# Work behind a unit's sums gets a smaller key in a list scheduler (four-layer graph network, one core)

## The chip, the cores and the metric

The kernel runs on one core of one Trainium2 chip. Five engines work from instruction queues of their own: TensorE (PE in the profile, with PEld for its weight loads), VectorE (DVE), ScalarE (ACT), GpSimd (POOL) and SyncE (SP), which here only issues DMAs. The metric is the device time of one launch, in microseconds (us). Six runs of the kernel before gave a median of 3188.3 us (3178.14 to 3199.47).

## The reference, cut to what matters

A batch of 8 graphs shares one adjacency matrix of 2048 nodes: random, symmetric, with every node its own neighbour, about 17 neighbours a node. Each node has 128 features in float32. Four layers follow each other: attention, graph, attention, graph.

```python
# layers 0 and 2 (8 heads of 16)
Q, K, V = h @ Wq, h @ Wk, h @ Wv
attn = softmax(where(adj == 0, -inf, Q K^T / sqrt(16)))
x = layer_norm(h + (attn V) @ Wo + bo, ln1_g, ln1_b)
x = layer_norm(x + relu(x @ W1 + b1) @ W2 + b2, ln2_g, ln2_b)   # 128 -> 256 -> 128
# layers 1 and 3
h = x @ W
e = leaky_relu((h @ a_src)[i] + (h @ a_dst)[j], 0.2)
y = softmax(where(adj == 0, -inf, e)) @ h + x
x = ln_gamma * (y - mean(y)) * rsqrt(var(y) + 1e-5) + ln_beta
```

## The kernel before, in words

**Tiling.** The 2048 nodes are cut into 32 units of 64 nodes. A unit's neighbours are never multiplied as a full matrix: their rows are fetched from a table in DRAM, five steps `t` a unit (TG = 5; four steps of two tiles of 128 neighbour rows, one step of a single tile). A row of the table holds what a neighbour gives in the next layer for all eight batches (K and V in attention; h and its score in a graph layer). The eight batches lie in two halves of four, on the upper and lower rows or side by side.

**An attention unit** (`attention`, L1693). For each of its five steps: POOL issues the gather of the neighbour rows into a `kv` buffer (L1671, six buffers); PE spreads the queries to the neighbour rows with a 0/1 matrix `hot` (L1734, into `qe`); DVE multiplies them with K (L1746) and reduces by head (L1753); ACT takes the exponential (L1763); the V rows are weighed with it, on POOL or for some steps on DVE (L1773, "weighing"); PE adds the weighed rows and the weights up by node, again with `hot` (L1805, into `acc` and `sums`). This add is the last reader of the `kv` buffer.

**Behind a unit's sums** (`after_attention`, L1855). DVE inverts the sums (L1863, L1864) and divides (L1870). Then: four transposes on PE (`ps_t`, L1482), a copy on ACT (L1471), the product with Wo (`ps_o`, L1505), the residual add on DVE (L1882), centring on PE (`ps_c`, L1495), squares on ACT (L1607), the root (L1617, L1618), the normalised rows (L1640), transposes and scale (`x1`, L1650), the product with W1 in two parts (`ps_f`, ReLU at L1902), the product with W2 (`ps_y`, L1912), the second residual add and a second norm, and the layer's result `xnew`. `keep` stores it to DRAM (SP, L1359). `project` multiplies it with the next layer's weights (`ps_p`, L1533 and L1535), copies the rows out (L1471), adds a small score strip on DVE (L1573) and stores the rows to the next layer's table (SP, L1593).

**A graph unit** (`graph`, L1932) gathers in the same way, scores on DVE (L1971, L1978), exponential on ACT (L1983), builds weights on DVE (L1993) and adds up on PE (L2009). Behind its sums (`after_graph`, L2068) come the inverse, a scale, the centred residual (L2099), one norm, and either store and projection for the next layer or, in the last layer, the store of the output (L2120).

**Before a unit** `fetch` (L1366) loads x (L1371) and, in an attention layer, the compressed `hot` rows (L1386) through SP; ACT unpacks them (L1393).

**What sets the order.** No order is written out by hand. Every piece of work is an `op` with its cost per engine, a key, and the buffers that it reads and writes. `Plan.order` (L670) simulates the engines: whenever one is free in that simulation, it takes the ready op with the smallest key, if a buffer is free for it. Buffers of the tags `kv`, `hot`, `x`, `q_sb` and `acc` go out strictly by key. Ops are issued in the order found, so every engine and every DMA queue has one fixed program order on the chip. All products but the sums and the spreads share two PSUM buffers (tag `m`). POOL's and DVE's weighings can't both be planned with the shared port.

**The keys.** A unit's base is 1000 x layer + 5 x unit. In an attention unit, step t has key = base + t: gather and spread at key - 6, exponential at key - 4, multiply, reduce and add at key, weighing at key + 1.5. The fetch is at base - 12, the unpacking at base - 8, the queries at base - 4. In a graph unit the gather is at key - 12, the score at key - 1, the exponential at key - 4. Inverse and division are at base. Everything behind them is at `key` as set by the line that the change touches, the two residual adds and the roots at `key - 2`.

**The seams between layers.** A gather of layer n + 1 needs the stored table rows of layer n. In a graph layer the first four units do the steps of paired tiles first; these gathers read only rows of units 0 to 29, the others wait for units 30 and 31 too. Unit 31 does the work behind its sums in two halves of two batches.

**Layer 0** also builds the lists of neighbours from the adjacency matrix, until about unit 20, beside its attention.

Of the kernel before, what the change touches and what calls it, by code (L numbers as in the profile page):

```python
# [34 lines left out]
TG = 5  # L35
# [564 lines left out]
class Plan:  # L600
# [36 lines left out]
    def op(self, costs, fn, key, reads=(), writes=(), joins=(), holds=(), shares=(), port=False, dma=0):  # L637


        o = Op({e: us * self.share for e, us in costs.items()}, fn, key, port, dma)  # L640
        shares = [*shares, *(c.whole for c in (*reads, *writes, *joins, *holds) if c.whole)]
        before = set()
        for c in reads:
            before.update(c.writers)
        for c in writes:
            before.update(c.writers)
            before.update(c.readers)
        for c in joins:
            before.update(c.readers)
        for c in reads:  # L650
            c.readers.append(o)
        for c in writes:
            c.writers, c.readers = [o], []
        for c in joins:
            c.writers.append(o)
        before.update(w for c in holds for w in [c.owner, *c.writers] if w)
        for c in dict.fromkeys([*writes, *joins, *reads, *holds, *shares]):
            if c.tag:
                if not c.owner:
                    c.owner = o  # L660
                    o.allocs.append(c)
                c.left += 1
                o.cells.append(c)
        for b in before:
            b.next.append(o)
        o.waits = len(before)
        o.behind = [c.owner for c in (*shares, *joins) if c.tag and c.owner is not o]
        self.ops.append(o)
# [96 lines left out]
def flat(ap):  # L765
    return ap if len(ap.shape) == 2 else ap.rearrange("p b d -> p (b d)")


class Sparse:
# [1085 lines left out]
    def after_attention(self, n, u, acc, sums, x, base):  # L1855
        L, hb = self.layers[n], self.HB
        op, count, cols = self.op, len(self.blocks), self.columns
        key = base + TG
        heads = slice(self.blocks.start * H, self.blocks.stop * H)
        rc = self.rows("rc", [P, hb * H], 1, H)  # L1860

        def inverse(e):
            e.tensor_scalar(rc.tile, sums.tile[:, heads], 1e-30, None, ALU.max)  # L1863
            e.reciprocal(rc.tile, rc.tile)  # L1864

        op({"DVE": 0.5}, inverse, base, reads=[sums], writes=[rc])
        a = self.rows("rows", [P, hb, P], 1, 1, name="a")

        def divide(e):
            e.tensor_tensor(  # L1870
                a.tile.rearrange("p b (h d) -> p (b h) d", d=HD),
                acc.tile[:, cols].rearrange("p (c d) -> p c d", d=HD),
                rc.tile.unsqueeze(2).to_broadcast([P, count * H, HD]),
                ALU.mult,
            )

        op({"DVE": 0.65}, divide, base, reads=[acc, rc], writes=[a])

        def add_to(r, ps, bias, other, key, of=lambda t: t):
            op(  # L1880
                {"DVE": 0.72},
                lambda e: e.scalar_tensor_tensor(r.tile, ps.tile, bias, of(other.tile), ALU.add, ALU.add),  # L1882
                key,
                reads=[ps, other],
                writes=[r],
            )

        at = self.rows("at", [P, CH], 1, P)
        ps = self.transposed(a, key, at)
        op(self.either(0.6, 0.68), lambda e, ps=ps: self.copy(e, at.tile, ps.tile), key, reads=[ps], writes=[at])  # L1890
        r = self.rows("r", [P, CH], 1, P, name="r1")
        ps = self.product(L["Wo"], at, key, "ps_o", r)
        add_to(r, ps, L["bo"], x, key - 2, lambda t: t[:, cols])
        normed = self.norm(self.centred(r, key), key)
        x1 = self.scaled(normed, L["ln1_g"], L["ln1_b"], "x1", key)
        hidden = self.rows("hidden", [P, FFN // P, CH], 2, P)
        for f in range(FFN // P):
            ps = self.product(L["W1"][:, f * P : (f + 1) * P], x1, key, "ps_f", hidden)

            def relu(e, f=f, ps=ps):  # L1900
                if e is self.nc.scalar:
                    e.activation(hidden.tile[:, f, :], ps.tile, AF.Relu, bias=L["b1"][:, f : f + 1])  # L1902
                else:
                    e.tensor_scalar(hidden.tile[:, f, :], ps.tile, L["b1"][:, f : f + 1], 0.0, ALU.add, ALU.max)

            op(self.either(0.7, 0.68), relu, key, reads=[ps], joins=[hidden])
        r = self.rows("r", [P, CH], 1, P, name="r2")
        ps = self.bank("ps_y")
        for f in range(FFN // P):
            op(  # L1910
                {"PE": 1.0},
                lambda e, f=f, ps=ps: e.matmul(  # L1912
                    ps.tile,
                    lhsT=L["W2"][:, f, :],
                    rhs=hidden.tile[:, f, :],
                    start=(f == 0),
                    stop=(f == FFN // P - 1),
                ),
                key,
                reads=[hidden],  # L1920
                writes=[ps],
                holds=[r],
            )
        add_to(r, ps, L["b2"], x1, key - 2)
        normed = self.norm(self.centred(r, key), key)
        x = self.scaled(normed, L["ln2_g"], L["ln2_b"], "xnew", key)
        self.keep(u, x, key)
        self.project(n + 1, u, x, key)
# [139 lines left out]
    def after_graph(self, n, u, outs, banks, acc, x, base):  # L2068
        L, hb = self.layers[n], self.HB
        op, cols, blocks = self.op, self.columns, self.blocks  # L2070
        key = base + TG

        rc = self.rows("rc", [P, hb], 1, 1, name="rcg")
        used = banks[blocks.start // 2 : blocks.stop // 2]
        outs = outs[blocks.start // 2 : blocks.stop // 2] if len(outs) > 1 else outs

        def inverse(e):
            for k, bank in enumerate(used):
                sums = bank()[:, 0 : 2 * (P + 1)].rearrange("p (b d) -> p b d", b=2)[:, :, P]
                e.tensor_scalar(rc.tile[:, 2 * k : 2 * k + 2], sums, 1e-30, None, ALU.max)  # L2080
            e.reciprocal(rc.tile, rc.tile)

        op({"DVE": 0.5}, inverse, base, reads=outs, writes=[rc])
        a = self.rows("rows", [P, hb, P], 1, 1, name="a")
        for k, b in enumerate(blocks):
            op(
                self.either(0.37, 0.28),
                lambda e, b=b, k=k: self.scale(e, a.tile[:, k, :], acc(b)[:, 0:P], rc.tile[:, k : k + 1]),
                base,
                reads=[*outs, rc],  # L2090
                joins=[a],
            )
        r = self.rows("r", [P, CH], 1, P)
        mine = x if self.made is None else Part(x, lambda t: t[:, cols])
        mine.writers = x.writers
        ps = self.centred(mine, key, r, a)
        op(
            {"DVE": 0.65},
            lambda e: e.tensor_tensor(r.tile, ps.tile, flat(a.tile), ALU.add),  # L2099
            key - 2,  # L2100
            reads=[ps, a],
            writes=[r],
        )
        normed = self.norm(r, key)
        if n < len(LAYERS) - 1:
            x = self.scaled(normed, L["ln_gamma"], L["ln_beta"], "xnew", key)
            self.keep(u, x, key)
            self.project(n + 1, u, x, key)
        else:

            def last(e):
                shape = [P, len(blocks), P]
                e.tensor_tensor(normed.tile, normed.tile, L["ln_gamma"].unsqueeze(1).to_broadcast(shape), ALU.mult)
                e.tensor_tensor(normed.tile, normed.tile, L["ln_beta"].unsqueeze(1).to_broadcast(shape), ALU.add)

            op({"POOL": 2.4, "DVE": 1.2}, last, key, writes=[normed], port=True)

            op(
                {"SP": 0.45},
                lambda e: e.dma_start(out=self.out[u][:, cols], in_=flat(normed.tile)),  # L2120
                key,
                reads=[normed],
                dma=P * P * 4 * len(blocks),
            )
# [105 lines left out]
```

## Time and profile before

| what | value |
| --- | --- |
| median of six runs | 3188.3 us (3178.14 to 3199.47) |
| the profiled execution: its time, its span | 3180.48 us, 3178.5 us |
| busy share of the span: PE, PEld, DVE, ACT, POOL | 76%, 44%, 72%, 45%, 67% |
| mean granted TensorE clock | 0.879 |
| moved by DMA | 1022.52 MB, mean 322 GB/s |
| gathers (POOL's queue), share of the 16 DMA engines | 72.8% |
| SP's queue, the same | 13.3% |

The times by stage follow from the traces of the gathers: layer 0 from 0 to about 1100 us, layer 1 to about 1655, layer 2 to about 2605, layer 3 to the end.

```profile
span 3178.5 us, 59465 instructions
...
DVE  7799889998889834444446888888988984555555
...
DMA  8788888999999769999987898999989967998994
...
L1671 POOL DMA_INDIRECT kv<-table,idx x1152 | 1196.6, 1039 | 826.2 <-issue 348.8
L1773 POOL TENSOR_TENSOR kv<-kv 128x2048 f32<-128x2048 f32 x260 | 921.1, 3555 | 63.9 <-ACT kv L1763 59.5
L1746 DVE TENSOR_TENSOR kv<-qe,kv 128x2048 f32<-128x2048 f32 (+1 forms) x320 | 662.0, 2069 | 114.4 <-DMA kv<-table,idx 60.8
L1753 DVE TENSOR_REDUCE s<-kv 128x128 f32<-128x2048 f32 (+1 forms) x320 | 659.6, 2061 | 9.0 <-DVE kv L1746 0.5
```

How to read it: the two rows of digits cut the span into 40 slices of 79.5 us; a digit is the busy share of the slice in tenths. DVE's row shows the four layers: 8 and 9 in the two attention layers, 4 and 5 in the two graph layers, where DMA's row has mostly 9. The last four lines are groups of instructions: line, engine, operation, what it writes and reads, count; then busy time, mean of one in ns; then the time its engine stood still just before them, and what ended most of it. DVE spends 1321.6 us of its 2302.6 us in the multiplies and reduces of the attention layers.

### The profile page before, as it was taken

The numbers are of one execution on the slowest core, as the hardware profiler recorded it, in microseconds if no ns is written. First come the engines' busy times: TensorE is split into PE (matmuls) and PEld (weight loads), VectorE is DVE, ScalarE is ACT, GpSimd is POOL, SyncE is SP. The second block draws the span as 40 slices with busy tenths as digits, with TensorE's granted clock in tenths as the row PEclk, the third lists the DMA queues.
The fourth block names the chain that finished last, engine by engine and source line by source line (L and its number), as shares of the span: only waits on it lengthen the run. The fifth ranks groups of instructions, "written<-read, shape, count | busy, mean of one in ns | idle before, by whom it ended". The sixth has DMA issues, their size and how long they took to land.

```text
span 3178.5 us, 59465 instructions
## 1 busy us (share of the span) xinstructions
PE 2419.4 (76%) x21668; PEld 1391.8 (44%) x21668; DVE 2302.6 (72%) x3783; ACT 1416.2 (45%) x4899; POOL 2130.9 (67%) x1456
## 2 busy tenths in 40 slices
PE   6667777777888758888885788788888786767774
PEld 4323333333344336665663333333333334555553
DVE  7799889998889834444446888888988984555555
ACT  5545555555444414444442344444444442433333
POOL 1388878988887645656554878878877865665552
PEclk8779989999999967888887999999999987887788
DMA  8788888999999769999987898999989967998994
GB/s 301 295 315 314 326 325 338 349 350 333 342 348 362 262 234 312 349 335 362 316 319 274 340 350 346 358 351 354 362 331 356 365 245 283 322 338 304 319 312 170
DMA packets 248061, 1022.52 MB, mean 322 GB/s; under 512 B 39184, under 2 KB 52880, under 8 KB 175856
## 3 DMA queue, kind: packets, MB, share of 16 engines
q0 software_dynamic: 166464, 864.44, 72.8%
q1 hardware_dynamic: 81296, 154.18, 13.3%
q8 instruction: 174, 2.85, 0.3%
q14 instruction: 127, 1.04, 0.1%
HBM read 978.23 MB, written 88.08 MB: 335 GB/s over the span
## 4 chain that ended last, share of the span: by engine, by line
PE 29%; DVE 12%; issue 10%; DMA 6%; POOL 4%; ACT 3%; another core or an unknown queue 3%; SPq 0%; POOLq 0%; DVEq 0%; ACTq 0%
DMA kv<-table,idx 5%; PE acc_q L2009 5%; DVE kv L1746 4%; PE qe L1734 3%; PE ps_c L1495 3%; PE sums L2009 3%; PE acc L2009 3%; PE ps_te L2032 2%; POOL kv L1671 2%; POOL kv L1773 2%; PE acc L1805 2%; DVE s L1753 2%; PE ps_p L1533 2%; PE ps_t L1482 1%
## 5 line engine op out<-in xcount | busy, mean ns | idle before, releaser
L1671 POOL DMA_INDIRECT kv<-table,idx x1152 | 1196.6, 1039 | 826.2 <-issue 348.8
L1773 POOL TENSOR_TENSOR kv<-kv 128x2048 f32<-128x2048 f32 x260 | 921.1, 3555 | 63.9 <-ACT kv L1763 59.5
L1746 DVE TENSOR_TENSOR kv<-qe,kv 128x2048 f32<-128x2048 f32 (+1 forms) x320 | 662.0, 2069 | 114.4 <-DMA kv<-table,idx 60.8
L1753 DVE TENSOR_REDUCE s<-kv 128x128 f32<-128x2048 f32 (+1 forms) x320 | 659.6, 2061 | 9.0 <-DVE kv L1746 0.5
L1734 PE MATMUL qe<-q_sb,hot 32*128 32x512 f32 (+1 forms) x2304 | 400.0, 698 | 168.1 <-DVE kv L1746 155.1
L1805 PE MATMUL acc<-kv,hot 128*32 128x512 f32 (+1 forms) x2304 | 363.5, 643 | 62.8 <-POOL kv L1773 33.7
L2009 PE MATMUL acc_q<-kv,w 128*32 128x129 f32 (+1 forms) x4608 | 274.6, 326 | 138.3 <-issue 93.5
L1993 DVE TENSOR_TENSOR w<-hot,e 128x512 f32<-128x512 f32 (+1 forms) x384 | 221.7, 597 | 211.4 <-remote 66.6
L2009 PEld LDWEIGHTS acc_q<-kv,w 128*32 128x32 f32 (+1 forms) x4608 | 187.9, 133 | 210.2 <-issue 146.4
L1734 PEld LDWEIGHTS qe<-q_sb,hot 32*128 32x128 f32 (+1 forms) x2304 | 106.6, 196 | 298.1 <-DVE kv L1746 223.8
L1763 ACT ACTIVATE kv<-s 128x128 f32<-128x128 f32 (+1 forms) x320 | 95.6, 299 | 306.8 <-DVE s L1753 191.9
L1607 ACT ACTIVATE junk<-ps_c 128x128 f32<-128x128 f32 x494 | 136.5, 276 | 183.1 <-PE ps_c L1495 135.1
L1471 ACT COPY trows<-ps_p 128x512 f32<-128x512 f32 (+1 forms) x237 | 112.4, 476 | 233.5 <-PE ps_p L1535 98.6
L1805 PEld LDWEIGHTS sums<-kv,hot 128*32 128x32 f32 (+1 forms) x2304 | 89.5, 118 | 206.6 <-issue 202.8
L1505 PE MATMUL ps_f<-x,W 128*128 128x512 f32 (+1 forms) x264 | 157.7, 683 | 28.0 <-ACT hidden L1902 14.2
L2009 PE MATMUL sums<-kv,w 128*32 128x129 f32 (+1 forms) x2304 | 152.8, 308 | 33.5 <-issue 32.9
L2009 PE MATMUL acc<-kv,w 128*32 128x129 f32 (+1 forms) x2304 | 139.6, 313 | 48.5 <-DVE w L1993 16.8
L1495 PE MATMUL ps_c<-centre,r 128*128 128x128 f32 x1024 | 151.4, 295 | 23.5 <-DVE r L1882 9.5
L1495 PEld LDWEIGHTS ps_c<-centre,r 128*128 128x128 f32 x1024 | 130.7, 200 | 65.5 <-DVE r L1882 29.5
L1912 PE MATMUL ps_y<-hidden,W 128*128 128x512 f32 (+1 forms) x264 | 143.1, 629 | 9.0 <-ACT hidden L1902 4.7
L1983 ACT ACTIVATE e<-e 128x16 f32<-128x16 f32 (+1 forms) x320 | 63.2, 210 | 189.7 <-DVE e L1978 139.8
L1902 ACT ACTIVATE hidden<-ps_f,b 128x512 f32<-128x512 f32 (+1 forms) x127 | 86.0, 677 | 137.6 <-PE ps_f L1505 95.2
(204 smaller groups left out, 3859.2 us busy)
## 6 DMA issues: line engine op xcount, KB each, us to landing
x<-xd SPq DMA_DIRECT2D x96, 256.0 KB
xd<-xnew SPq DMA_DIRECT2D x93, 256.0 KB
kv<-table,idx POOLq DMA_INDIRECT x1152
table<-trows SPq DMA_DIRECT2D x128, 130.0 KB
kv<-adj_dram SPq DMA_DIRECT2D x16, 1024.0 KB
table<-trows SPq DMA_DIRECT2D x32, 512.0 KB
table<-trows SPq DMA_DIRECT2D x64, 256.0 KB
kv<-xk_dram SPq DMA_DIRECT2D x8, 1024.0 KB
```

The lines of the kernel that those rows point to most:

```text
L1495: e.matmul(ps.tile[:, cols], lhsT=flat(x.tile)[:, cols], rhs=self.centre, start=True, stop=True)
L1505: lambda e: e.matmul(ps.tile, lhsT=w, rhs=x.tile, start=True, stop=True),
L1607: e.activation(self.junk, x, AF.Square, scale=P**-0.5, accum_out=var.tile[:, b, 1:2])
L1671: e.indirect_dma_start(out=rows(kv.tile, j), out_offset=None, in_=self.tables[n][0:nodes], in_offset=bass.IndirectOffsetOnAxis(ap=self.idx ...
L1734: e.matmul(qe.tile[:, j, hf, :], lhsT=hot.tile[rows, t * P : (t + 1) * P], rhs=q.tile[rows, :], start=True, stop=True,)
L1746: e.tensor_tensor(k, qe.tile[:, 0:tiles].rearrange("p j h c -> p (j h) c"), k, ALU.mult)
L1753: e.tensor_reduce(s.tile[:, 0 : tiles * heads].rearrange("p (q c) -> p q c", q=2 * tiles), k, axis=mybir.AxisListType.X, op=ALU.add,)
L1773: e.tensor_tensor(v, v, w.unsqueeze(3).to_broadcast([P, 2 * tiles, heads // 2, HD]), ALU.mult)
L1805: e.matmul(out[rows, :], lhsT=hot.tile[:, col : col + GROUP * (3 - tiles)], rhs=rhs[:, 2 * j + hf, :], start=(t == 0), stop=(t == TG - 1),)
L1912: lambda e, f=f, ps=ps: e.matmul(ps.tile, lhsT=L["W2"][:, f, :], rhs=hidden.tile[:, f, :], start=(f == 0), stop=(f == FFN // P - 1),),
L1993: e.tensor_tensor(w.tile[:, :, j : j + tiles, :].rearrange("p x j c -> p j x c"), oh[:, j : j + tiles].unsqueeze(2).to_broadcast(shape), e ...
L2009: e.matmul(acc(b)[at : at + GROUP * (3 - tiles), :], lhsT=w.tile[:, hf * hb + b, j : j + 3 - tiles, :].rearrange("p j c -> p (j c)"), rhs= ...
```

## The change

```diff
     def after_attention(self, n, u, acc, sums, x, base):
         L, hb = self.layers[n], self.HB
         op, count, cols = self.op, len(self.blocks), self.columns
-        key = base + TG
+        key = base + TG - 5
...
     def after_graph(self, n, u, outs, banks, acc, x, base):
         L, hb = self.layers[n], self.HB
         op, cols, blocks = self.op, self.columns, self.blocks
-        key = base + TG
+        key = base + TG - 5
```

In both functions the key of everything behind the division (or the scale) goes from base + 5 to base, and that of the residual adds and the roots from base + 3 to base - 2. Base + 5 is the next unit's base. So the moved ops were ranked with the next unit's multiply of its first step; now they are ranked with the first multiply of their own unit, ahead of the next unit's spreads from its third step on (base + 1 to base + 3), its exponentials (base + 1 to base + 5), a graph unit's scores (base + 4 on) and its queries (base + 1), and ahead of the unpacking for the unit after next (base + 2). The fetch for the unit after next has base - 2. Inverse and division stay at base. Nothing is computed differently; only the order in which the planner takes ready work changes, with a few ops that may run on ACT or DVE, and one weighing, on another engine.

## The prediction, on record before the result

> **What bounds the kernel now.** I read the busy shares over the span first, then busy time by stage (fixed stretches of the trace), then the waits of each engine inside a stage, then the events around the two hand-overs from an attention layer to a graph layer.
>
> The table by stage: stretch, length, then busy time of PE, PEld, DVE, ACT, POOL, granted TensorE clock, DMA share, GB/s.
>
> ```profile
> 760.00:1080.00 320.00, 263.16 (x1825) 125.28 (x1827) 277.42 (x209) 145.65 (x499) 262.02 (x146) 0.93 0.91 348
> 1080.00:1200.00 120.00, 72.80 (x605) 46.05 (x597) 60.99 (x135) 34.22 (x124) 46.84 (x45) 0.75 0.58 207
> 1730.00:2580.00 850.00, 683.24 (x4807) 317.43 (x4806) 730.21 (x543) 377.78 (x1288) 683.21 (x383) 0.96 0.91 349
> 2720.00:3120.00 400.00, 290.09 (x4018) 222.00 (x4013) 211.25 (x695) 150.08 (x612) 238.03 (x225) 0.78 0.91 320
> ```
>
> Row 3 is layer 2: DVE is busy 730.21 of 850 us (86%), ahead of PE and POOL (80% each). The stretch repeats every four units, 112 us, and about 98 us of each are DVE's, so a unit costs 28 us and only some 3.5 us of that is DVE idle. Row 1, the end of layer 0, is alike (87%). Row 4, the last layer, has DVE at 53% and DMA at 0.91: gathers bound it. Row 2 is a hand-over, where nothing is full (DVE 51%, DMA 0.58).
>
> In layer 2 the waits say what DVE, ACT and POOL stand still for (engine, line, what it waited for: us, times, longest):
>
> ```profile
> DVE kv L1773 <- ACT ps_e L1763: 25.1, 6, 8.9
> DVE r L1882 <- PE ps_o L1505: 21.7, 7, 5.4
> DVE kv L1746 <- PE qe L1734: 18.6, 12, 5.3
> ...
> ACT hot L1393 <- DMA hot<-hots: 50.0, 13, 5.8
> ...
> POOL kv L1671 <- PE sums L1805: 23.5, 10, 6.5
> ```
>
> Each engine takes its instructions in one fixed order. A wait in it is a consumer put too soon after its producer: `r L1882` (first residual add) after the product with Wo, the cast L1393 after the fetch of the compressed rows, a gather L1671 after the add that frees its buffer. The reader is to see that these sums are gaps on engines that are the bound or feed it, and that the change shifts exactly these distances.
>
> The first hand-over (start, length, engine line, operation, tiles):
>
> ```profile
> 1123.33 1.09 SPq L1593 DMA_DIRECT2D table<-trows  x2
> ...
> 1127.24 1.02 POOL L1671 DMA_INDIRECT kv<-table,idx  x1 [32.75 <-issue]
> ...
> 1162.05 2.31 PE L2032 MATMUL ps_te<-t,hot 128*128 128x16 f32 x10 [20.11 <-ACT hidden L1902]
> ...
> 1186.37 1.49 SPq L1593 DMA_DIRECT2D table<-trows  x2
> ```
>
> POOL stands 32.75 us, until unit 29's rows are stored at 1123.33; only then may the first gather of layer 1 start. Unit 31's rows, which the rest needs, come at 1186.37. At the second hand-over the pair is 2612.49 and 2616.47, with 6.54 us of POOL standing still.
>
> **The change, part by part.** No arithmetic is added or removed. What follows comes from the instruction order of the two programs, with durations from the trace. What moves is everything behind the division: per attention unit 29 PE instruction groups (12 transposes, Wo, W1 twice, W2 twice, 8 centrings, 4 projections: 3x0.6+1.1+2x1.1+2.1+2x1.1+1.4 = 10.8 us), 28 on ACT (11.3 us), two residual adds and two spreads on DVE (2x0.75+2x0.15 = 1.8 us), and on SP one store of x and two of table rows. They now come ahead of the next unit's later spreads (L1734), exps (L1763) and graph scores, and on SP ahead of or nearer to the fetches of the unit after next (L1371, L1386). On POOL the gathers shift against the weighings.
>
> (a) First hand-over. In the old order unit 29's two projections follow the fifth, last add (L1805) of unit 31 on PE; in the new one they follow the second. Three adds are about 15 us at the pace of the last unit, so unit 29's store and the first gather move from 1127.24 to about 1112. But unit 30's chain now starts later against the last add, as unit 29's holds the two banks, and unit 31's chain comes last as before: its store at 1186 need not move. In the 34 us after the first gather:
>
> ```profile
> 1127.00:1161.00 34.00, 9.47 (x62) 6.80 (x62) 6.48 (x21) 5.58 (x21) 23.79 (x24) 0.60 0.94 364
> ```
>
> 24 gathers fill the DMA engines (0.94) and PE does 9.47 us of work: `ps_te L2032` follows 20.11 us of nothing. If that standstill moves forward with the gathers, it falls on unit 31's last adds and the saving is eaten. Bounds: the whole 15 us saved, or 0. I take -8, the middle, as nothing decides. The instruction queues q8 and q14 carry one or two packets in this window, so code loading behind some 12 MB of gathers (364 GB/s for 34 us) may be the standstill; the row doesn't prove it.
>
> The Trainium skill, "Runtime: NRT & Kernel Launch", section "Instruction fetch mechanics", has the sequencer prefetch 16 KiB pages of code over its own DMA queue, so that crossing a page is mostly hidden. That speaks against the row of 20.11 us being code; by the rule the gathers would cost other work nothing and term (a) would be -15, by the row at its worst 0. It stays outside the sum.
>
> (b) Second hand-over. There the old order already had the projections between the second and third add, so the gather gains at most 2 us (2616.47), while unit 30's chain, formerly at W2 by the last add, is now at its first centring: two products, two hidden tiles and a norm later, 2x1.1+2x0.7+2.1+about 4 = 10 us. Bounds -2 and +10; I take +3, nearer the lower: in the stretch of the first hand-over no engine passes 61%, so a later chain can be made up.
>
> (c) Casts behind fetches. A fetch takes from 2193.56 to 2203.22, 9.6 us:
>
> ```profile
> 2193.56 0.42 SPq L1386 DMA_DIRECT2D hot<-hots  x1
> ...
> 2203.22 0.99 ACT L1393 CAST hot<-hot 128x960 f32<-128x960 fp8e5 x1 [5.15 <-DMA hot<-hots]
> ```
>
> In the last units of layer 0 the old order leaves 7.7 to 14.9 us of DVE work between fetch and cast. In the new one the fetch stands behind the table store on SP, and 3.9, 8.3, 8.9, 7.1, 12.1, 7.7 and 2.7 us are left: against 9.6 us that is short by 5.7+1.3+0.7+2.5+0+1.9+6.9 = 19 us. Behind the waiting cast queue ACT's exps, and behind them the weighings of POOL and DVE. Bounds 0 and 19; ACT is at 46% there and catches up part: +9. In layer 2 the same sum falls from 43 (the trace has 50.0) to 32: 0 to -11, I take -4.
>
> (d) Residual adds behind Wo. Between the division L1870 and `r L1882` lie a transpose, a copy and the product: by the trace about 7 us. DVE's own work put between the two has a mean of 8.0 us in layer 2 before, 18 of 31 units at 7; after, 6.45, with 15 units at 4 to 5. In layer 0 the mean goes from 12.95 to 9.5, with 8 units at 5 or less where there was none. Short by about 2.3 us in 23 units: 15x2.3+8x2.3 = 34+18 = 52 us of DVE idle if none of it would have been idle anyway. The old order's seven waits cost 21.7 us, 3.1 each, so such waits are real; but DVE already idles 3.5 us a unit, and a wait here makes the next one shorter (PE and POOL run on). Bounds 0 and +52; I take a third, +18, because two thirds of the old gaps lie at other lines (25.1+18.6 against 21.7) and can be absorbed.
>
> (e) Gathers behind adds. In layer 2 the POOL work between a weighing and the gather that reuses its buffer grows from a mean of 4.71 to 5.77 us, with gathers that have under 4 us falling from 68 to 48 of 116. The trace charges 23.5 us to `sums L1805`. Bounds -16 (48/68 left: 23.5x20/68 = 7, and as much in layer 0, where the mean goes from 4.61 to 5.23) and 0, as POOL isn't the bound: -6.
>
> (f) Graph layers. The after-work is smaller, DMA is at 0.91, DVE and ACT have room; what hides the shift is the gathers' transfer. Uncovered it would be a score's delay per unit; I take 0, with 8 us to either side (a quarter us in each of 32 units).
>
> Sum: -8+3+9-4+18-6+0 = +12. The profiled execution has a span of 3178.5 and took 3180.5 us, so 3192.5 on its scale. It lies 7.8 below the median of the six runs (3188.3), so on that scale 3200.
>
> **The rivals.** Forecast: the added waits on DVE and ACT outweigh the earlier gather, 3193 to 3220, centre 3200.
>
> Rival 1, faster: the first hand-over keeps its 15 us, POOL's freer gathers give 10 and the casts of layer 2 4, while (d) is absorbed in idle that was there anyway and (c) costs 4: -25, 3163. For it: the gap of 32.75 us is on POOL with nothing else to do, and DVE has 14% idle. Against it: unit 31's store, not unit 29's, releases the rest of the gathers.
>
> Rival 2, no change: the moved work lies beside a bound engine and every stage keeps its pace, 3188. For it: the multiply, the reduce and the DVE weighing dominate DVE's order and hardly move (between a reduce and its weighing 3.56 us before, 4.07 after). Against it: (a) and (d) are each larger than what can be told.
>
> Rival 3, much slower: the standstill behind the first 24 gathers lands on unit 31's last adds and on the chains of units 30 and 31 at both hand-overs, some 20 us each (the row of 20.11): +40, with (c) and (e) at +9-4-6 = -1 and (d) absorbed: 3227. It decides from the point where the first gather is issued before unit 31's last spread. For it: the window row above. Against it: at the second hand-over the gathers hardly move.
>
> **How the numbers follow.** The six runs spread over 21 us; about 0.3%, 9.6 us, is what can be told from no change: faster is under 3178.7, slower over 3197.9. Forecast 0.44 (slower 0.34, same 0.10); rival 1 0.29 (faster 0.27, same 0.02); rival 2 0.17 (same 0.13, faster 0.02, slower 0.02); rival 3 0.10 (slower). Together faster 0.29, same 0.25, slower 0.46. The time is the forecast's, 3200, whose own range is 3190 to 3220. The whole range goes down to rival 1 (3162) and up to rival 3 (3228); the lower bounds of all terms together (-52) and the upper (+89) would need every cover to fail at once and lie outside.
>
> **What would show it.** (a) The first gather of layer 1 near 1112, and whether unit 31's store comes before 1186: if it comes 15 us sooner, rival 1; if the standstill lies in unit 31's adds, rival 3. (b) The second pair of stores 60 us apart as before, or more. (c) Waits of the cast on `hot<-hots` between 760 and 1080. (d) Waits of `r L1882` on `ps_o` in layer 2 well above 21.7 us, and a period above 112 us; an unchanged period and sum would refute my main term. (e) POOL's gathers waiting less than 23.5 us on `sums`. I am wrong if layer 2 gets shorter between its first and last gather, since then the shorter distance to Wo costs nothing.

## The result, and the profile after

The changed kernel takes 3209.64 us (median of 20 runs, 3194.79 to 3224.31), the one before 3188.57 us (46 runs): a ratio of 1.0064, 95% interval 1.0049 to 1.0079. It is slower by some 20 us. The forecast was slower by 12, to 3200, with a range of its own from 3190 to 3220: direction and range held, and the 12 forecast are somewhat over half of what was measured.

The page of the changed kernel, the lines that answer to those of before (its profiled execution took 3213.7 us, 4 above its median; that of before lay 8 below):

```profile
span 3212.0 us, 59470 instructions
...
L1773 POOL TENSOR_TENSOR kv<-kv 128x2048 f32<-128x2048 f32 x259 | 917.6, 3554 | 129.4 <-ACT kv L1763 124.4
L1746 DVE TENSOR_TENSOR kv<-qe,kv 128x2048 f32<-128x2048 f32 (+1 forms) x320 | 662.9, 2072 | 171.1 <-DMA kv<-table,idx 82.5
```

The same work takes the same time (3554 against 3555 ns a weighing, 2072 against 2069 a multiply). What grew is the idle time ahead of it. POOL stands 129.4 us before its weighings, 124.4 of them for the exponentials; before the change 63.9 and 59.5. DVE stands 171.1 us before its multiplies; before, 114.4.

One stretch of the table by stage, the columns as in the prediction:

```profile
760.00:1080.00 320.00, 260.71 (x1751) 123.26 (x1755) 270.15 (x207) 147.32 (x493) 251.90 (x140) 0.91 0.87 328
```

All three busy engines and DMA do less in the same 320 us (DVE 270.15 against 277.42, POOL 251.90 against 262.02, DMA 0.87 against 0.91). That fits a slower layer 0, but a fixed stretch lies earlier in the work of the slower kernel, so its sums can't be laid on each other; stages have to be cut by events. I cut at the first residual of a graph layer's units (L2099), which comes when an attention layer is quite over:

| us | to unit 20's division in layer 0 | to the first residual of layer 1 | layer 1, first to last residual | from there to the first residual of layer 3 | rest | span |
| --- | --- | --- | --- | --- | --- | --- |
| before | 810.5 | 1202.5 | 488.4 | 1001.5 | 486.1 | 3178.5 |
| after | 837.0 | 1229.7 | 481.5 | 1018.6 | 482.2 | 3212.0 |
| difference | +26.5 | +27.2 | -6.9 | +17.1 | -3.9 | +33.5 |

The losses are in the two attention layers and their hand-overs; the graph layers gain a little. In layer 0 the loss is there by unit 20 in this profile, while the lists are still being built. Each row is one execution.

The waits in layer 2 after the change, the columns as in the prediction, from 1800 to 2550 us (over that stretch the kernel before has the sums that the prediction shows, only 16.4 us for the spread):

```profile
DVE kv L1746 <- DMA kv<-table,idx: 31.4, 17, 5.5
DVE kv L1746 <- PE qe L1734: 18.5, 17, 5.9
...
DVE r L1882 <- PE ps_o L1505: 4.1, 3, 2.1
...
ACT hot L1393 <- DMA hot<-hots: 17.4, 8, 3.9
...
POOL kv L1671 <- PE sums L1805: 28.8, 21, 3.2
```

The wait that the prediction built its largest term on, the residual add for the product with Wo, went down, from 21.7 to 4.1 us. In its place DVE's multiply waits for its gather: 31.4 us, against 3.6 before. Cut by events, from the first to the last division of layer 2, the two go from 21.7 to 5.6 us and from 4.3 to 35.0.

The first hand-over after the change:

```profile
1142.92 1.09 SPq L1593 DMA_DIRECT2D table<-trows  x2
...
1146.89 1.02 POOL L1671 DMA_INDIRECT kv<-table,idx  x1 [4.41 <-issue]
...
1156.80 0.69 DVE L1870 TENSOR_TENSOR a<-acc,rc 128x256 f32<-128x256 f32 x2
...
1214.01 1.09 SPq L1593 DMA_DIRECT2D table<-trows  x2
```

The first gather of layer 1 now comes 10 us ahead of layer 0's last division (1156.80) where it came 5 us behind it (1127.24 against 1121.94): 15 us earlier in relation to it, as worked out. But unit 31's rows come 57 us after that division, against 64 before, and all of it sits on a layer 0 that ends 35 us later.

### The profile page after: what moved, and what is told of

Same layout as the page of the kernel before. It is cut to its first block, busy times and chain, and to the rows that moved or that the text cites. A ratio compares the mean times of both kernels' runs of the same rounds, so it can differ in the third digit from the quotient of the medians.

```text
span 3212.0 us, 59470 instructions
## 1 busy us (share of the span) xinstructions
PE 2439.1 (76%) x21668; PEld 1396.3 (43%) x21668; DVE 2317.9 (72%) x3790; ACT 1416.0 (44%) x4893; POOL 2120.9 (66%) x1455
## 5 line engine op out<-in xcount | busy, mean ns | idle before, releaser
L1773 POOL TENSOR_TENSOR kv<-kv 128x2048 f32<-128x2048 f32 x259 | 917.6, 3554 | 129.4 <-ACT kv L1763 124.4
L1746 DVE TENSOR_TENSOR kv<-qe,kv 128x2048 f32<-128x2048 f32 (+1 forms) x320 | 662.9, 2072 | 171.1 <-DMA kv<-table,idx 82.5
L1734 PE MATMUL qe<-q_sb,hot 32*128 32x512 f32 (+1 forms) x2304 | 407.1, 713 | 160.6 <-DVE kv L1746 150.0
L1805 PE MATMUL acc<-kv,hot 128*32 128x512 f32 (+1 forms) x2304 | 370.5, 656 | 68.8 <-POOL kv L1773 45.9
L2009 PE MATMUL acc_q<-kv,w 128*32 128x129 f32 (+1 forms) x4608 | 285.1, 323 | 156.6 <-issue 114.8
L1471 ACT COPY trows<-ps_p 128x258 f32<-128x258 f32 (+1 forms) x235 | 111.8, 476 | 244.7 <-PE ps_p L1535 118.4
L1805 PEld LDWEIGHTS sums<-kv,hot 128*32 128x32 f32 (+1 forms) x2304 | 91.1, 120 | 214.1 <-issue 208.7
L2009 PE MATMUL sums<-kv,w 128*32 128x129 f32 (+1 forms) x2304 | 145.8, 306 | 34.8 <-issue 34.8
L1505 PE MATMUL ps_f<-x,W 128*128 128x512 f32 (+1 forms) x264 | 155.7, 677 | 12.4 <-ACT x L1650 10.1
L1805 PEld LDWEIGHTS acc<-kv,hot 128*32 128x32 f32 (+1 forms) x2304 | 56.1, 116 | 217.5 <-issue 108.4
L1482 PE MATMUL ps_t<-ident,normed 128*128 128x128 f32 x638 | 118.4, 314 | 38.9 <-DVE normed L1642 10.7
```

The source lines that it names most:

```text
L1482: e.transpose(ps.tile[:, b * P : (b + 1) * P], flat(x.tile)[:, b * P : (b + 1) * P], self.ident)
L1505: lambda e: e.matmul(ps.tile, lhsT=w, rhs=x.tile, start=True, stop=True),
L1734: e.matmul(qe.tile[:, j, hf, :], lhsT=hot.tile[rows, t * P : (t + 1) * P], rhs=q.tile[rows, :], start=True, stop=True,)
L1746: e.tensor_tensor(k, qe.tile[:, 0:tiles].rearrange("p j h c -> p (j h) c"), k, ALU.mult)
L1773: e.tensor_tensor(v, v, w.unsqueeze(3).to_broadcast([P, 2 * tiles, heads // 2, HD]), ALU.mult)
L1805: e.matmul(out[rows, :], lhsT=hot.tile[:, col : col + GROUP * (3 - tiles)], rhs=rhs[:, 2 * j + hf, :], start=(t == 0), stop=(t == TG - 1),)
```

## The experiments

The runs were made in three groups, on chips other than that of the result. The kernel before took 2933.7, 2934.4 and 3158.8 us on them, so only ratios within a group, and stages of runs with the kernel before at the same level, are compared.

### First group: which layer, and a control

```diff
e1_att0     after_attention:  key = base + TG - (5 if n == 0 else 0)
e2_att2     after_attention:  key = base + TG - (5 if n == 2 else 0)
e3_graph    after_graph:      key = base + TG - 5
e4_quarter  both:             key = base + TG + 0.25
```

> Only layer 0's after-work gets the smaller key. Theory Q (PE runs the moved products ahead of the next unit's spreads, ACT the moved squares ahead of the next unit's exponentials, so DVE's multiplies and POOL's weighings wait; the traces put +35 us of the +33.5 into layer 0 and give 8 back at the first hand-over): 12 to 30 us slower than before, 3200 to 3218. Rival D (the prediction's residual adds put too soon behind Wo): 8 units short of 2.3 us, at most +18, and the waits of r L1882 on ps_o in layer 0 grow by as much. Rival C (any reshuffle of the order moves the time by this much, with no mechanism of its own): anywhere from -20 to +20, with no tie to qe and exponentials.

> Only layer 2's after-work gets the smaller key. Theory Q: the traces have +12 us inside layer 2 and +7 at the second hand-over, so 5 to 20 us slower. Rival D: the larger half of the loss is here (15 units against 8), 15 to 34 us slower, and more than with layer 0 alone. Rival C: no tie to either.

> Only the two graph layers' after-work gets the smaller key. Theory Q: DVE, PE and ACT have room there, the gathers bound it; the traces have -7 us in layer 1 and -4 in layer 3: 0 to 10 us faster, or no change. Rival D: no change, the graph layers have no product with Wo. Rival C: -20 to +20.

> Control: the key of the after-work of all layers is a quarter of a step larger, which only turns ties. It measures how far a reshuffle alone moves the time. Theories Q and D: within 0.3% of before (3179 to 3198). Rival C: as far off as the change itself, 15 us or more to either side.

| run | ratio to before (95%) | unit 20 | first residual of layer 1 | layer 1 | to layer 3 | rest |
| --- | --- | --- | --- | --- | --- | --- |
| e1_att0 | 1.0069 (1.0045 to 1.0092) | 819.1 | 1192.1 | 404.0 | 966.5 | 382.7 |
| e2_att2 | 1.0069 (1.0044 to 1.0093) | 805.0 | 1169.3 | 405.2 | 987.6 | 382.8 |
| e3_graph | 0.9989 (0.9975 to 1.0003) | 805.4 | 1173.3 | 405.0 | 964.2 | 384.8 |
| e4_quarter | 1.0066 (1.0044 to 1.0087) | 816.1 | 1174.7 | 403.5 | 981.6 | 384.1 |

e2 and e3 leave layer 0 in the old order and e1 and e3 leave layer 2 in it, so the old order's stages are known twice on this chip: 1169 and 1173, 967 and 964. These two profiles agree within some 4 us; how far others would lie apart isn't known. The change costs 19 to 23 us in layer 0 (14 of them by unit 20) and 21 to 23 in layer 2. Rival D's claim that layer 2 takes more than layer 0 fails; the two are equal. In layer 0 its waits of the residual add for the product with Wo did grow, from 1.0 and 3.4 us (e3, e2) to 9.9 (e1), which is half of the loss at most; in layer 2 they fell (e2: 6.1, against 21.3 in e3). The graph layers give nothing that can be told from none here.

The control is the run to remember. A quarter of a step turns ties (and in layer 0 also lets list work go first whose keys lie 0.1 or 0.2 higher). Theories Q and D gave it at most 0.3%; it costs 1.0066, as much as either layer, as Rival C had it. Its loss is nearly all in the stage of layer 2 (+16). So a loss of this size can't by itself be taken as proof of any mechanism: the order of before is one that other orders of the same work rarely reach. But it isn't the same loss. Of the 16 us, 10 arise at the second hand-over and 4 to 6 in layer 2 itself; the change's loss there is the other way round, as the second group shows.

### Second group: which engine's part

Which op a key outranks is decided on that op's engine alone, so the change can be cut by engine. In p_pe only ops with a cost on PE get the smaller key, in p_act only those that may run on ACT. (Cut to SP's ops alone, the smaller key leaves the planned order of every engine as it was, so there was nothing to run.)

```diff
p_all   the changed kernel
p_pe, p_act   in Plan.op, for ops behind the division ('PE' for p_pe, 'ACT' for p_act):
-        o = Op({e: us * self.share for e, us in costs.items()}, fn, key, port, dma)
+        o = Op({e: us * self.share for e, us in costs.items()}, fn, key - 5 * (self.behind and 'PE' in costs), port, dma)
p_q     the changed kernel, and
-            op({"PE": 1.2}, spread, key - 6, ...
+            op({"PE": 1.2}, spread, key - 11, ...
-            ... exp(e, exps(kv)), key - 4, ...      (and the second exponential of L1763)
+            ... exp(e, exps(kv)), key - 9, ...
```

> The changed kernel itself, on the chip of this group, as the whole that the parts are held against. Theory Q and the two single layers before it (1.0069 each, graph layers 0.9989): 1.008 to 1.014 of before. Rival C (every reshuffle costs about the same 0.7%, as the quarter step's 1.0066 did): 1.004 to 1.009, no sum of the layers.

> Only the ops of the after-work that run on PE get the smaller key (transposes, products, centrings, projections), all layers; those of ACT, DVE and SP keep theirs. Theory Q, PE side (products ahead of the next unit's spreads): most of the loss is here, 1.006 to 1.012, with more waits of the multiply on qe in layer 0 (traces: 7 us before, 25 with layer 0 changed). Theory Q, ACT side: under 1.003. Rival C: about 1.007 whatever the part.

> Only the ops of the after-work that run on ACT, or on ACT or DVE by choice, get the smaller key (copies, squares, scales, ReLU). Theory Q, ACT side (squares ahead of the next unit's exponentials, so POOL's weighing waits, and the gather behind it on POOL is late): most of the loss is here, 1.006 to 1.012, with the weighing's waits on exponentials in layer 0 well above the 11 us of before. Theory Q, PE side: under 1.003. Rival C: about 1.007 whatever the part.

> The changed kernel, with the spreads and the exponentials of the attention layers five steps earlier too, so that they keep their old rank against the after-work on PE and ACT, while the after-work still goes ahead of adds, casts, scores and multiplies. Theory Q: the loss is gone, 0.995 to 1.003 of before, first gathers of layer 1 as early as in the changed kernel. Rival D (residual adds behind Wo) and the casts behind fetches: the loss stays, 1.006 or more. Rival C: about 1.007 again.

| run | ratio to before (95%) | unit 20 | first residual of layer 1 | layer 1 | to layer 3 | rest |
| --- | --- | --- | --- | --- | --- | --- |
| p_all | 1.0114 (1.0090 to 1.0137) | 818.1 | 1188.9 | 403.3 | 986.3 | 381.0 |
| p_pe | 1.0065 (1.0044 to 1.0086) | 821.2 | 1200.0 | 404.0 | 974.6 | 383.3 |
| p_act | 1.0240 (1.0217 to 1.0264) | 819.3 | 1201.8 | 405.3 | 1004.3 | 383.0 |
| p_q | 1.0057 (1.0037 to 1.0077) | 825.8 | 1194.7 | 404.9 | 981.1 | 383.1 |

The whole is the product of its layers (1.0069 x 1.0069 x 0.9989 = 1.0127 against 1.0114), so the loss isn't a constant that any reshuffle pays once. The engines' parts don't add: ACT's alone costs twice the whole, PE's alone half of it. Neither side of theory Q has the loss to itself, since each left the other under 1.003; ACT's part is the dear one, above all in layer 2 (1004 against some 965). Giving spreads and exponentials their old rank halves the loss but doesn't end it, against Theory Q's 0.995 to 1.003; the total is also what Rival C said (about 1.007), so it decides nothing by itself. The rows of p_q and p_all are from executions 14 us above and 9 us below their medians, so their columns can't be subtracted to a few us.

Taken apart, the stage of layer 2 says more:

| run | layer 2, first to last division | from there to the first residual of layer 3 |
| --- | --- | --- |
| e1_att0, e3_graph (order of before) | 853.1, 851.0 | 52.0, 53.2 |
| e2_att2, p_all (the change) | 871.0, 873.9 | 55.0, 52.9 |
| e4_quarter | 856.6 | 63.0 |
| p_pe | 856.1 | 57.1 |
| p_act | 885.4 | 58.9 |
| p_q | 853.5 | 67.7 |

The change loses its 18 to 23 us inside the layer, and with the old rank of spreads and exponentials (p_q) the layer takes its old time again, though this execution lay above its kernel's median. That is Theory Q, shown for layer 2 by one execution each. The same holds for layer 0 behind the lists: from unit 20's division to the last one it takes 300 and 304 us in the old order (e2, e3), 319 and 317 with the change (e1, p_all), 306.5 in p_q. What p_q doesn't bring back is the list part before unit 20 (825.8 against 805), and at the second hand-over it loses 15 us of its own. The control, in turn, loses mostly where the change does not.

The same stretch of layer 2 in the columns of the prediction's table, for e3_graph, p_all and p_q:

```profile
1638.30:2489.30 851.00, 708.22 (x4954) 329.62 (x4955) 750.62 (x577) 396.33 (x1345) 692.77 (x387) 0.96 0.91 350
...
1651.80:2525.70 873.90, 709.07 (x4965) 334.97 (x4966) 761.21 (x583) 393.92 (x1343) 691.99 (x389) 0.94 0.89 343
...
1659.60:2513.00 853.40, 701.29 (x4934) 329.16 (x4934) 751.86 (x576) 393.31 (x1337) 688.86 (x382) 0.95 0.90 347
```

Of the 23 us that p_all adds to e3_graph, DVE is busy for 10.6 (761.21 against 750.62; 2.3 of them are one weighing that the plan took from POOL) and idle for the other 12.3. p_q is back at both.

One rival isn't tested: the granted TensorE clock. Over this stretch of layer 2 it is 0.96 to 0.97 in the four profiles of the old order and 0.93 to 0.95 in all others. Runs of one kernel with a lower mean clock are longer too: by a straight line, 1.8 us for each 0.001 in the 33 runs of the kernel before in the third group, 1.3 in those of the changed kernel on the chip of the result. So part of a loss may go with the clock, as cause or as consequence. In layer 2 p_q speaks against it as the whole cause: 0.95, and the old time.

Groups of DVE in layer 2, old order (e3_graph) and then the changed one (p_all); the last columns are the idle time just before the group and what ended it:

```profile
L1746 DVE TENSOR_TENSOR kv<-qe,kv 128x2048 f32<-128x2048 f32 (+1 forms) x152 | 313.6, 2063 | 22.8 <-PE qe L1734 13.7 <-DMA kv<-table,idx 8.7
L1773 DVE TENSOR_TENSOR kv<-kv,ps_e 128x1024 f32<-128x1024 f32 (+1 forms) x38 | 53.5, 1409 | 33.2 <-ACT ps_e L1763 33.2
L1882 DVE SCALAR_TENSOR_TENSOR r<-ps_o,bo,x 128x512 f32<-128x512 f32 x31 | 23.1, 745 | 21.3 <-PE ps_o L1505 21.3
```

```profile
L1746 DVE TENSOR_TENSOR kv<-qe,kv 128x2048 f32<-128x2048 f32 (+1 forms) x152 | 314.3, 2068 | 73.0 <-DMA kv<-table,idx 37.7 <-PE qe L1734 27.3 <-PE ps_t L1482 3.4
L1773 DVE TENSOR_TENSOR kv<-kv,ps_e 128x1024 f32<-128x1024 f32 (+1 forms) x38 | 53.5, 1408 | 2.3 <-ACT ps_e L1763 2.3
L1882 DVE SCALAR_TENSOR_TENSOR r<-ps_o,bo,x 128x512 f32<-128x512 f32 x31 | 23.1, 745 | 6.2 <-PE ps_o L1505 6.0
```

The three idle times add up to 77 us before and 82 after. At these lines DVE didn't get many new waits; they changed place, from the weighing and the residual add to the multiply, that is to the gather and the spread of the next unit. Nor is the idle time before the multiply the loss as such. In p_q, whose layer 2 takes its old time, it is longer still:

```profile
L1746 DVE TENSOR_TENSOR kv<-qe,kv 128x2048 f32<-128x2048 f32 (+1 forms) x152 | 314.2, 2067 | 87.3 <-DMA kv<-table,idx 47.1 <-PE qe L1734 32.6 <-PE ps_p L1535 4.8
```

The residual add waits less because its producers moved forward with it: from the end of the division to the end of the product with Wo I count 8.2 us on average over 31 units in e3_graph and 6.3 in p_all, and at the end of layer 0 (from unit 20) 13.4 and 7.2.

In layer 0 one of the larger single losses can be read in the events of p_all (start, length, engine, line, tiles, idle before):

```profile
674.10 0.74 DVE L1882 SCALAR_TENSOR_TENSOR r<-ps_o,bo,x 128x512 f32<-128x512 f32 x1
684.95 0.19 DVE L1863 TENSOR_SCALAR rc<-sums 128x32 f32<-128x32 f32 x1 [10.10 <-PE sums L1805]
...
681.74 1.94 POOL L1773 TENSOR_TENSOR kv<-kv 128x1024 f32<-128x1024 f32 x1
...
679.04 1.16 PE L1826 MATMUL ps_q<-Wq,x 128*128 128x128 f32 x8
685.73 2.09 PE L1734 MATMUL qe<-q_sb,hot 32*128 32x512 f32 x8
```

DVE has done the unit's last reduce and a residual add and then stands 10.1 us, until POOL has weighed the last step (681.74 + 1.94) and PE has added it. Nothing of the next unit is there to fill the time: its queries only run at 679.04 and its first spread at 685.73, behind the after-work that now goes first. The changed kernel's own run has the same event (11.0 us). In the old order (e3_graph) the next unit's first spread runs well ahead of the same unit's inverse, two more follow it (678.27 and 682.57), and DVE comes to the inverse without a wait:

```profile
674.44 1.14 PE L1734 MATMUL qe<-q_sb,hot 32*128 32x512 f32 x8
...
687.02 0.18 DVE L1863 TENSOR_SCALAR rc<-sums 128x32 f32<-128x32 f32 x1
```

### Third group: the other neighbours, and the gain alone

```diff
x_exps      the changed kernel, exponentials (L1763) at key - 9 in place of key - 4
x_all       the same, and spreads at key - 11, queries and their copy at base - 9 in place of base - 4
x_all_cast  the same as x_all, and the unpacking (L1393) at key - 1 in place of key + 4
x_seam27g   the kernel before, and
-        key = base + TG                                            (after_attention)
+        key = base + TG - (5 if n == 0 and u >= 27 else 0)
-        key = base + TG                                            (after_graph)
+        key = base + TG - 5
```

> The changed kernel with spreads, exponentials and the next unit's queries of the attention layers all five steps earlier (the run before left the queries behind the after-work). That run brought layer 2 back to 853 us and the end of layer 0 (from unit 20 on) to 306, but not the part of layer 0 that builds the lists (826 at unit 20 against 805). Theory Q': the queries, which need one of the two shared PSUM buffers that the after-work now takes first, are what is late there: unit 20's division back at 805 to 810 and the whole at 0.996 to 1.002 of before. Rival C' (in the list part any other order of the same work costs 11 to 21 us, as it did in all five orders tried so far, the quarter step among them): unit 20 stays at 815 or later, the whole at 1.004 to 1.007.

> As the run beside it, with the unpacking of the compressed rows five steps earlier too. Theory of the casts (the prediction's term (c)): another 3 us or more off layer 0 and layer 2. Theory Q': no more than 0.1% from the run beside it. Rival C': unit 20 at 815 or later again.

> The changed kernel with only the exponentials of the attention layers five steps earlier; spreads and queries stay behind the after-work. It tells ACT's queue from PE's. Moving ACT's part alone cost layer 2 33 us and PE's part 4. Theory ACT: layer 2 goes back to 851 to 857 us (changed kernel: 874), first seam stays at 54; the whole 1.004 to 1.007. Theory PE (the spreads): layer 2 stays at 868 to 876.

> The smaller key only where the runs showed a gain: in layer 0 for units 27 to 31, and in the graph layers; the rest is as before. Theory Q with the prediction's term (a): layer 0 as before (1105 to 1112 us to its last division), the way from there to the first residual of layer 1 at 54 instead of 64, layer 2 as before: 0.994 to 0.997 of before, faster than both kernels. Rival: the gain at the hand-over was bought by the later end of layer 0, and what is earlier there is late here: 0.998 to 1.002.

| run | ratio to before (95%) | unit 20 | first residual of layer 1 | layer 1 | to layer 3 | rest |
| --- | --- | --- | --- | --- | --- | --- |
| x_exps | 0.9977 (0.9956 to 0.9999) | 810.5 | 1190.5 | 475.6 | 1012.1 | 471.5 |
| x_all | 0.9980 (0.9956 to 1.0003) | 828.7 | 1203.1 | 470.8 | 999.7 | 469.5 |
| x_all_cast | 0.9994 (0.9972 to 1.0015) | 793.7 | 1202.9 | 480.5 | 1003.4 | 473.2 |
| x_seam27g | 0.9921 (0.9896 to 0.9946) | 803.0 | 1182.9 | 477.3 | 993.5 | 466.2 |

The order of before isn't profiled on this chip; x_seam27g has it in layer 0 up to unit 26 and in layer 2, and stands in for it there.

All three kernels with the exponentials' old rank are back at the kernel before or a trace faster. How much that recovers isn't known, since the changed kernel itself wasn't run on this chip; it cost 1.0064 and 1.0114 on others. (p_q, with 1.0057, had that rank too. It ran where the graph layers gain least; against the whole beside it, 1.0114, it recovered half.) x_exps does it with the exponentials alone, better than the 1.004 to 1.007 that Theory ACT gave it. At the first residual it is 8 us behind x_seam27g (1190.5 against 1182.9). In layer 2 it is Theory PE that holds: from first to last division the layer takes 878 us in x_exps against 863 in x_seam27g, and only with spreads and queries at their old rank too does it come back, to 855 in x_all and 859 in x_all_cast. These two then lose 15 us at the second hand-over (84 and 85 against 69.5), as p_q did; why is open. The casts add nothing that can be told, 0.9994 against 0.9980, but the intervals are as wide as the 9 us of the prediction's term. In the list part of layer 0, unit 20's division came at 793.7, 810.5 and 828.7 us in these three, with no tie to what was restored: Theory Q' fails there, and Rival C' too, since x_all_cast beats the old order by 9 us at that point and loses it again by the end of the layer.

x_seam27g is faster than the kernel before: 0.9921, more than the 0.994 to 0.997 expected (and so faster than the changed one, which was slower than the kernel before on both chips where it ran). Its first hand-over:

```profile
1099.59 1.09 SPq L1593 DMA_DIRECT2D table<-trows  x2
...
1103.51 2.80 POOL L1671 DMA_INDIRECT kv<-table,idx  x1 [6.70 <-PE ps_f L1505]
...
1139.05 0.42 DVE L1473 COPY at<-ps_t 128x256 f32<-128x256 f32 x1 [16.04 <-remote]
...
1139.53 1.12 PE L1482 MATMUL ps_t<-ident,normed 128*128 128x128 f32 x4 [14.84 <-issue]
...
1167.31 1.09 SPq L1593 DMA_DIRECT2D table<-trows  x2
...
1171.04 0.99 POOL L1671 DMA_INDIRECT kv<-table,idx  x1 [16.35 <-DMA table<-trows]
```

Unit 29's rows are stored at 1099.59 and POOL stood 6.70 us for them, not 32.75. Unit 31's come at 1167.31, 52 us after its division (64 before the change). The way from the last division to the first residual of layer 1 took 67.7 us, not the 54 expected. The two middle rows hold a good part of that: in the midst of the first 24 gathers DVE stood 16.04 us and PE 14.84, and the profile shows no instruction that they waited for. It looks like the prediction's row of 20.11 us, and it lies where Rival 3 put it, in the chains of units 30 and 31; no run shows what stands behind it.

The 25 us gained (0.79% of 3158.8) come from this seam, the graph layers and whatever else the new order brings; the parts weren't run alone. By the traces of other chips the seam's own gain is 3 to 6 us, and the graph layers' is 11 on one chip and not told from none on another. So how the 25 divide is open.

## Why the prediction was right, and where it wasn't

**Direction and size.** Slower was right, and 3209.6 lies in the forecast's own 3190 to 3220. The terms gave +12, the two medians +21, the two profiled executions +33.5. That the sum came near is partly luck: the largest term had the wrong sign in the layer where it was mostly to arise, and in the profile 26.5 of the 33.5 us were lost by unit 20, where no term stood.

**(a) First hand-over, -8.** The moved gather came as worked out, 15 us earlier against the layer's last division. What it brought, from unit 26's division to the first residual of layer 1, is 3 us on the chip of the result (223.8 to 221.0) and 5 to 6 in the first group (203 and 204 in the old order, 198 with layer 0 changed), inside the bounds but below the value taken. The reason is the one named: unit 30's chain starts later. Its rows are stored 47 us after the last division (1203.48), against 17 before (1138.65).

**(b) Second hand-over, +3.** From the last division of layer 2 to the first residual of layer 3 it is 73 us after against 68 before on the chip of the result; in the first two groups 55 and 53 with the change against 53 and 52: right in size.

**(c) Casts, +9 and -4.** In the late part of layer 0 the waits on the fetch went from 1.3 to 9.5 us, and in layer 2 from 50.0 to 17.4: the two signs were right. What they did to the time isn't shown; x_all_cast finds no gain from the cast's old rank, within an interval as wide as the term.

**(d) Residual adds, +18: the step that failed.** The prediction took the "about 7 us" between division and product with Wo from the old order and held the new order's shorter cover against it. That time isn't a property of the chain: most of it was waiting for other work of PE and ACT, and the change moves just that. It fell with the cover (8.2 to 6.3 us in layer 2, 13.4 to 7.2 at the end of layer 0); the shortest in layer 2 went from 5.1 to 2.6. In layer 2, where the term put 34 of its 52 us of shortage, the wait went from 21.7 to 4.1 us, about -18 at that line. In layer 0 it grew, from 2.7 to 6.8 on the chip of the result and from 1.0 and 3.4 to 9.9 and 9.1 in the first two groups: sign and size right there. The layer's period did get longer, as the prediction's sign asked, but with the sum falling it was not for this reason. (By the row of the table DVE is busy for 96 us of 112, not 98, so its idle time was 4 us a unit rather than 3.5.)

**What stood in its place.** The prediction listed that the after-work goes ahead of the next unit's spreads and exponentials, and then priced neither, nor the queries. Over the span the multiplies' idle time grew by 57 us and that of POOL's weighings by 65, by the page, while that of other lines shrank. That their rank is the loss is shown inside layer 2, and in layer 0 behind the lists: both are back, or nearly, in p_q, and layer 2 again in x_all. For the list part of layer 0 it isn't shown. Layer 0 as a whole cost 27 us (16 to 23 in the other groups) where the terms had about +4 (-8+9+6-3), with 26.5 of it by unit 20 on the chip of the result, in a part that no term covered.

**(e) Gathers, -6.** The gain didn't come: waits on `sums L1805` in layer 2 went from 23.5 to 28.8 us over the fixed stretch, from 33 to 32 between its first and last division, and in layer 0 from 31.6 to 41.5; gathers came late for the multiply (3.6 to 31.4). Work counted between a weighing and its gather says nothing when the weighing itself is late. (The bound of -16 is -14 by its own numbers, twice 7.)

**(f) Graph layers, 0.** They gained 11 us in the two profiled executions of the result, a trifle outside the 8 allowed. One profile each is thin for that: layer 1 alone ranges over 10 us among the four kernels of the third group. Where gathers run faster (405 against 488 us a layer) the gain is 0.1% and not told from none.

**The rivals.** Of Rival 1's parts, the hand-over gained, but 3 to 6 us in place of 15, and the freer gathers didn't come; x_seam27g shows that seam and graph layers together do gain (0.9921), but in the whole change the attention layers took back more. Rival 2 is out, with 1.0064 and an interval above 1. Rival 3's condition wasn't met: the first gather (1146.89) came behind unit 31's last spread (1141.1). Two of that unit's adds (1147.35 and 1150.39) still lay behind it, and PE had no gap above 4 us in the 34 us that followed. In x_seam27g the standstill did come, 14.84 us of it.

**What stays open.** Why the lists' part of layer 0 swings between 794 and 829 us at unit 20 from one order to the next, which holds most of the loss on the chip of the result; why the second hand-over loses 10 to 15 us in the control and with the restored ranks; and how much of it all goes with the granted clock. Shown are the place (both attention layers, half each in the first group), the exchange of waits on DVE, and that inside layer 2 the old rank of spreads and exponentials brings the old time back.

## What to carry to other kernels

In a list schedule a moved group takes its own producers along, so a distance read from the old order can't be held against the new one; price instead what it is moved past, op by op on each engine, here the spreads, exponentials and queries that feed the bound engine's next unit. Run a control that hardly does more than turn ties before reading a mechanism into half a per cent: here it cost as much as either layer's share. Then look where it loses, with stages cut by events: equal totals came from different places. And where a change gains at a seam and loses in the steady part, apply it at the seam alone.

## What the runs showed of the hardware

The same program took 3188 us on the chip of the result and 2934, 2934 and 3159 us in the three groups. The difference lies mostly in the graph layers: layer 1 from first to last residual took 488 us in the old order there, 403 to 405 in the first two groups, in any order, and 471 to 480 in the third, where all four kernels have the smaller key in the graph layers; meanwhile the attention layers, in which DVE is the busiest engine, differed by 3 to 4% (1001.5 against 964 to 967 us for layer 2). From 1200 to 1560 us, inside layer 1, the traces show 339 GB/s moved on the chip of the result, 406 in the first group (e2_att2) and 349 in the third (x_exps). So what an edit in the graph layers is worth may depend on the chip it is measured on.
